# Naming ScalarE's function tables, and reading the shift weights from PSUM, in a decoder layer whose order is written by a planner

## The chip, the cores and the metric

The kernel runs on one core of a Trainium2 chip. Its time is the device time of one execution in microseconds (us). A core has a matrix engine (TensorE, PE in the profile), a vector engine (VectorE, DVE), an engine for functions such as exp and sqrt (ScalarE, ACT), a general engine (GpSimd, POOL) and a sync engine (SP) that only issues transfers. Each engine runs its own list of instructions in the order in which the program gives them; semaphores make one engine wait for another. Matrix products land in a memory of their own, PSUM, of which the kernel uses eight banks of 128x512 float32; the other memory on the core is SBUF, and in this kernel GpSimd reads and writes only that.

## The reference

One decoder layer over x of 16 sequences, 256 steps, 256 channels, all float32. It has three parts, each followed by a residual sum and a layer norm:

```python
# 1. gated cosine/sine recurrence
z = causal_conv4(x @ in_proj_w) + conv_b          # values, gate, 32 scores
p_w = exp(clip(score_scale * s_raw, -20, 20)) * time_weight
re, im = cumsum(p_w * poly(x5) * cos(x5 * theta)), cumsum(p_w * poly(x5) * sin(x5 * theta))
y = rms_normalised(re, im) @ (W_re, W_im)
x = layernorm(x + (y * silu(gate)) @ out_proj_w)
# 2. attention over shifts in time, 16 heads of 16 channels
corr = irfft(rfft(Q) * conj(rfft(K))).mean(channels)
w, idx = top_k(corr, 5);  w = softmax(w)
x = layernorm(x + sum_k(w[k] * V rolled by idx[k]) @ Wo + bo)
# 3. eight experts, forward and inverse branch
h = gelu(Q @ router_w1.T + b1);  weights = softmax(h @ router_w2.T + b2)
out = sum_k(weights[k] * ((Q @ V[k]) * cumsum(K @ W[k])) @ U[k].T) / n_valid
x = layernorm(x + out)
```

## The kernel before, in words

The 16 sequences are worked on as 8 pairs. For every pair the program notes seven stages (lines 1202 to 1204): `front` and `body` (part 1), `context`, `back` and `attention` (part 2), `router` and `experts` (part 3). Nothing is issued while a stage is noted. `Later` (line 68) and `Work.note` (line 186) put each instruction into a list with an estimate of its duration, the tiles that it touches and what it depends on. `Work.run` (line 424) then plans: `forward` (line 267) hands out work engine by engine by rank and readiness, `backward` (line 414) makes new ranks from the latest starts, this is done three times, and the order with the shortest planned span is kept. `give` (line 435) issues the instructions in that order. All of them are issued from line 438, so the profile puts nearly everything on L438, and an operation is known by its tiles.

Three things of the planner bear on the change.

- **Tables.** The planner takes ScalarE to hold one set of functions at a time. `SETS` (line 120) tells the planner which functions share one: Exp 0, Sin and Silu 1, Gelu 2, Sqrt 3. When the function kind changes, `forward` adds 1283 ns (lines 372 and 373). The kernel issues no load of a table; whatever builds the program puts one in where a function needs it.
- **Places.** A tile takes one of its tag's buffers when its first instruction is planned, and gives it back after its last. For a tile in a PSUM pool with several buffers, `after` (filled at line 259) lists the SBUF tiles that its readers use; `room` (line 289) lets the first product into the bank only if there are places for those as well, and `takes` (line 409) only if what the readers depend on is already planned.
- **Locks.** Two-input VectorE and GpSimd instructions on SBUF are planned so that they don't overlap (`lock`, lines 177 and 376). One with a PSUM operand is planned without that.

The planner keeps no order between two engines that only read the same PSUM tile.

The part of the data path that changes is in attention. For each pair `choose` (line 955) picks five shifts for 32 heads, transposes their weights (`w_t_ps`, `wT`) and turns them into weights per frequency by 12 small products into a bank `w_f_ps`, one of the four banks of the pool `f_ps` that also carries `c_ps`, `v_ps`, `u_ps`, `h_ps`, `kv_ps`, `q_ps`, `roll_ps` and others. ScalarE copies its 96 columns to SBUF, tile `wf`. `rolled` (line 1002), once for each sequence of the pair, multiplies the spectrum `vf` of V by these weights into tile `t`: two 128x256 products on VectorE, two on GpSimd, then two sums on VectorE, and 16 products into two `roll_ps` banks. There is one buffer for `t`, shared with `pp`: the second sequence of a pair can write its `t` only when the first one's `roll_ps` products have read theirs. `layernorm` (line 559) uses Sqrt, `front` Exp and Silu, `body` Sin and Sqrt, `choose` Exp, `router` Gelu and Exp.

Of the kernel before, what the change touches and what calls it, by code (L numbers as in the profile page):

```python
# [18 lines left out]
PSUM = bass.MemoryType.PSUM  # L19
HBM = bass.MemoryType.DRAM  # L20

P = 128
# [5 lines left out]
NH, DK = 16, 16  # L28
# [20 lines left out]
EARLY, SLABS, XT_BUFS, ZC_BUFS, KBUFS, VBUFS, X_BUFS = 3, 18, 1, 6, 2, 3, 9  # L49
AHEAD = range(1, NP)  # L50
PH_BUFS = 2
# [62 lines left out]
class Work:  # L114
# [3 lines left out]


    SETS = {AF.Exp: 0, AF.Sin: 1, AF.Silu: 1, AF.Gelu: 2, AF.Sqrt: 3}  # L120
    AHEAD = 40000.0
    LEAD = {"PE": 0, "DVE": 85, "ACT": 103, "POOL": 40, "SP": 0}
    LATE = {"PE": 33, "DVE": 35, "ACT": 35, "POOL": 80, "SP": 40}
# [62 lines left out]
    def note(self, eng, op, issue, args, kw):  # L186
# [21 lines left out]
        if op == "activation":  # L208
            o.table = self.SETS.get(args[2])
        for ap in ins + [out]:  # L210
# [26 lines left out]
    def prepare(self):  # L237
        for o in self.ops:
            if o.eng == "PE":
                cells, begin, end = {}, 0.0, 0.0  # L240
                for d, group in o.mm:
                    begin = max([begin] + [cells.get(g, 0.0) for g in group])
                    cells.update((g, begin + d) for g in group)
                    end, begin = max(end, begin + d), begin + 13
                o.dur, o.lat = end, end + 165
            for q in o.pre:
                q.then.append(o)
        self.slots, self.turn, self.kind, self.after = {}, {}, {}, {}
        for name, (t, users) in self.tiles.items():
            users[:] = dict.fromkeys(users)  # L250
            self.slots.setdefault(t.tag, t.tag_meta.bufs)


            kind = t.tag, t.source_name if t.source_name in self.shares else None
            self.kind[name] = None if t.space == PSUM and t.tag_meta.bufs > 1 else kind
            if self.kind[name]:
                self.turn.setdefault(kind, []).append(name)
            to = [n for o in users if o.eng != "PE" for n in o.tiles if n != name] if not self.kind[name] else []
            self.after[name] = [n for n in dict.fromkeys(to) if self.tiles[n][0].space != PSUM]

    def gap(self, q, o, raw):

# [4 lines left out]
    def forward(self, rank, late=None):  # L267
        need = {o: len(o.pre) for o in self.ops}

        ready = {o: max(0.0, late[o] - self.AHEAD) if late and o.fetch else 0.0 for o in self.ops}  # L270
        can = {e: sorted((rank[o], o.k, o) for o in self.ops if o.eng == e and not o.pre) for e in self.LEAD}
# [161 lines left out]
        self.give(best[1], best[2])  # L433

    def give(self, order, starts):
        for o in order:
            for call, args, kw in o.parts:
                call(*args, **kw)  # L438

# [2 lines left out]
def decoder_kernel(ctx: ExitStack, tc: tile.TileContext, a: dict, out: bass.AP):  # L442
    nc = tc.nc
    ctx.enter_context(tc.manual_schedule())
    work = Work(1)
    work.shares.update({"raw": 11, "inv": 2, "ks": 6, "ct": 2, "bothc": 1, "specc": 2, "e": 8, "wb": 3, "h": 2, "lT": 1, "lg8": 1, "fwT": 2, "x": 3, "dx": 2, "x2": 4})
    V, S, G, T, Y = (
        Later(work, name, eng)
# [38 lines left out]
    def split(ps, n=2):  # L487
        return ps.rearrange("p (c d) -> p c d", c=n)
# [96 lines left out]
    spectra_of = {}  # L585
# [191 lines left out]
    ps = f_bank("bv_ps")  # L777
# [110 lines left out]
    def context(p):  # L888

        for b in (2 * p, 2 * p + 1):  # L890
# [3 lines left out]
            cf = transform(ct, G, "c", slab)  # L894
            if p in AHEAD:
                kf, vf = (slab([P, 2, D], "ks") for _ in range(2))
# [58 lines left out]
    def choose(prod):  # L955


        NHP = 2 * NH
        ps = f_bank("corr_ps")
        for i in range(3):  # L960
            T.matmul(ps[:NHP, :L], prod[:, i, :], c_corr[:, i, :], start=i == 0, stop=i == 2)
        T.matmul(ps[:NHP, L : L + 1], prod[:, 0, :], c_mean, start=True, stop=True)
        corr = new(at, [NHP, L], "corr")
        top = new(at, [NHP, 8], "top")
        m8 = new(at, [NHP, 8], "m8")
        rest = new(at, [NHP, L], "rest")
        S.copy(corr, ps[:NHP, :L])
        S.copy(top[:, 0:1], ps[:NHP, L : L + 1])
        V.max(m8, corr)
        V.tensor_copy(m5[:, :TOPK], m8[:, :TOPK])  # L970
        V.match_replace(rest, m5, corr, -FAR)
        V.tensor_scalar(m8, m8, top[:, 0:1], None, ALU.add)
        V.tensor_scalar(top[:, 1:2], m8[:, 0:1], -1.0, None, ALU.mult)
        V.tensor_tensor(top[:, 2:3], top[:, 1:2], top[:, 0:1], ALU.add)
        S.activation(m8, m8, AF.Exp, bias=top[:, 1:2])
        S.activation(corr, corr, AF.Exp, bias=top[:, 2:3])
        V.tensor_reduce(top[:, 3:4], m8[:, :TOPK], AX.X, ALU.add)
        V.reciprocal(top[:, 4:5], top[:, 3:4])
        V.scalar_tensor_tensor(corr, rest, -FAR, corr, ALU.is_equal, ALU.mult)

        we = new(at, [NHP, 2, P], "we")
        r = top[:, 4:5]
        S.activation(corr[:, P:], corr[:, P:], AF.Identity, scale=r)
        V.scalar_tensor_tensor(we[:, 0, :], corr[:, :P], r, corr[:, P:], ALU.mult, ALU.add)
        V.scalar_tensor_tensor(we[:, 1, :], corr[:, :P], r, corr[:, P:], ALU.mult, ALU.subtract)
        ps = f_bank("w_t_ps")
        for c in range(2):
            T.transpose(ps[:, c * NHP : (c + 1) * NHP], we[:, c, :], ident[:NHP, :NHP])
        wT = new(at, [P, 2, NHP], "wT")
        S.copy(wT, split(ps[:, : 2 * NHP]))  # L990
        ps = f_bank("w_f_ps")
        for i in range(3):
            for o in range(2):
                T.matmul(
                    ps[64 * o : 64 * o + 64, i * NHP : (i + 1) * NHP], f_roll[:, o, i, :], wT[:, o, :],
                    start=True, stop=True,
                )
        wf = new(at, [P, 3, NHP], "wf")
        S.copy(wf, split(ps[:, : 3 * NHP], 3))
        return wf  # L1000

    def rolled(b, vf, wf):

        lo = (b % 2) * NH

        def times(eng, dst, f, kind):
            eng.tensor_tensor(
                dst.rearrange("p (h d) -> p h d", d=DK),
                vf[:, f, :].rearrange("p (h d) -> p h d", d=DK),
                wf[:, kind, lo : lo + NH].unsqueeze(2).to_broadcast([P, NH, DK]),  # L1010
                ALU.mult,
            )

        t = new(at, [P, 4, D], "pp", name="t")
        times(V, t[:, 0, :], 0, 0)
        times(G, t[:, 1, :], 1, 2)
        times(G, t[:, 2, :], 1, 1)
        times(V, t[:, 3, :], 0, 2)
        V.tensor_tensor(t[:, 0, :], t[:, 0, :], t[:, 1, :], ALU.add)
        V.tensor_tensor(t[:, 2, :], t[:, 2, :], t[:, 3, :], ALU.subtract)  # L1020
        banks = [f_bank("roll_ps") for o in range(2)]
        work.apart()
        work.joins = True
        for cb in range(2):
            for i in range(2):
                for o in range(2):
                    rows = slice(64 * o, 64 * o + 64)
                    T.matmul(
                        banks[o][:, cb * P : (cb + 1) * P], t[rows, 2 * i, cb * P : (cb + 1) * P], c_roll[rows, i, :],
                        start=i == 0, stop=i == 1,  # L1030
                    )
        work.joins = False
        work.apart()
        aT = new(at, [P, 2, L], "aT")
        for o in range(2):
            S.copy(aT[:, o, :], banks[o][:, :L])

        ps = f_bank("wo_ps")
        for o in range(2):
            for cb in range(2):  # L1040
                T.matmul(ps[:, o * D : (o + 1) * D], aT[:, o, cb * P : (cb + 1) * P], wo[:, cb, :], start=cb == 0, stop=cb == 1)
        dx = xs[b]
        V.tensor_tensor(dx, dx, split(ps), ALU.add)
        x = xs[b] = new(mx, [P, 2, D], "x", X_BUFS, "x2")
        G.tensor_tensor(x[:, 0, :], dx[:, 0, :], dx[:, 1, :], ALU.add)
        G.tensor_tensor(x[:, 1, :], dx[:, 0, :], dx[:, 1, :], ALU.subtract)

    def attention(p):
        place = lambda f: work.place("att", p, f)
        work.rank = place(0.0)  # L1050
        prod = new(at, [P, 3, 2 * NH], "prod", 2)
        pair = (2 * p, 2 * p + 1)
        for b in pair:
            work.rank = place(0.15 * (b % 2))
            spectra(b, prod)
        work.rank = place(0.4)
        wf = choose(prod)
        for b in pair:
            work.rank = place(0.7 + 0.15 * (b % 2))
            rolled(b, spectra_of[b][1], wf)  # L1060
        work.rank = place(1.0)
        layernorm(at, "al", [xs[b][:, c, :] for b in pair for c in range(2)], b_eps4)

# [283 lines left out]
```

## Time and profile before

| what | us |
|---|---|
| time, median of 3 runs | 868.76 (867.9 to 875.24) |
| the profiled execution | 868.91 |
| its span | 867.1 |
| PE busy | 812.6 (94%) |
| DVE busy | 712.3 (82%) |
| ACT busy | 593.4 (68%) |
| POOL busy | 273.4 (32%) |

The mean clock granted to TensorE was 0.985 of full speed. The span is what the trace covers; the profiled execution's own time is 1.8 us longer. Busy times overlap and don't add up to the span. In a group's line the fields are: engine, operation, output and input tiles, shapes, count, then total busy us and mean ns of one instruction, then the idle time of that engine just before these instructions with the releaser that ended most of it. In a line of waits the three numbers are the total us, how often, and the longest one.

### The profile page before, as it was taken

How to read it: one execution, taken by the hardware profiler on the slowest of the kernel's cores; microseconds unless marked ns; L12 is line 12 of the kernel's file. 1: busy time of each engine (PE TensorE's matmuls, PEld its weight loads, DVE VectorE, ACT ScalarE, POOL GpSimd, SP SyncE). 2: the span in 40 equal slices, each digit the busy share in tenths (PEclk: the TensorE clock that was granted, in tenths of full speed). 3: DMA queues.
4: the chain of work that ended last, by engine and by line, in shares of the span. 5: the costliest groups of instructions: out<-in, count | busy, mean ns of one | idle time of the engine just before them, and what ended most of it. 6: DMA issues, size and time to landing. Idle time of an engine off the chain costs nothing.

```text
span 867.1 us, 12898 instructions
## 1 busy us (share of the span) xinstructions
PE 812.6 (94%) x4628; PEld 464.9 (54%) x4628; DVE 712.3 (82%) x1248; ACT 593.4 (68%) x884; POOL 273.4 (32%) x301
## 2 busy tenths in 40 slices
PE   4799998899989999999999999899999999999994
PEld 2355553554435655565446654565566457556553
DVE  6499799779999999999899999999999985472331
ACT  3769968489978689748878787889875824532301
POOL 8522386535113123250232321353334221130000
PEclk9899998999999999999999999999999999999997
DMA  8963657255726442744075435535544340040130
GB/s 274 325 129 71 182 168 222 77 146 134 185 52 154 102 106 65 179 121 99 25 175 142 101 83 133 140 82 108 149 97 96 69 116 1 3 119 1 39 83 24
DMA packets 52304, 99.16 MB, mean 114 GB/s; under 512 B 6592, under 2 KB 18912, under 8 KB 52240
## 3 DMA queue, kind: packets, MB, share of 16 engines
q1 hardware_dynamic: 42640, 67.65, 34.0%
q0 software_dynamic: 9600, 30.69, 10.9%
q8 instruction: 36, 0.59, 0.3%
q14 instruction: 28, 0.23, 0.1%
HBM read 28.06 MB, written 11.53 MB: 46 GB/s over the span
## 4 chain that ended last, share of the span: by engine, by line
PE 54%; DVE 22%; ACT 9%; issue 6%; DMA 6%; SPq 2%; POOL 1%; POOLq 0%; DVEq 0%; ACTq 0%
PE u_ps L438 9%; PE v_ps L438 9%; PE c_ps L438 9%; DVE cs L438 7%; PE h_ps L438 5%; DVE sn L438 3%; PE kv_ps L438 3%; DVE zc L438 3%; PE in_ps L438 3%; PE wo_ps L438 2%; PE out_ps L438 2%; DMA sn<-zc 2%; PE q_ps L438 2%; SPq L438 2%; PE y L438 2%
## 5 line engine op out<-in xcount | busy, mean ns | idle before, releaser
L438 ACT ACT_TABLE_LOAD x96 | 123.2, 1283 | 41.4 <-DVE flmv L438 36.5
L438 PE MATMUL v_ps<-fxT,w_v 128*128 128x512 f32 x256 | 119.5, 600 | 1.2 <-ACT e L438 1.2
L438 PE MATMUL c_ps<-fcT,w_c 128*128 128x512 f32 x256 | 119.0, 599 | 0.7 <-DVE e L438 0.7
L438 PE MATMUL u_ps<-u_o,e 128*128 128x256 f32 x512 | 116.7, 381 | 0.6 <-DVE e L438 0.6
L438 PEld LDWEIGHTS u_ps<-u_o,e 128*128 128x128 f32 x512 | 95.7, 190 | 19.0 <-issue 6.3
L438 DVE TENSOR_TENSOR_SCAN cs<-again,cs 128x1024 f32<-128x1024 bf16 x32 | 82.0, 2564 | 0.0
L438 DVE SCALAR_TENSOR_TENSOR zc<-in_ps,pv,zc 128x255 f32<-128x255 f32 (+4 forms) x144 | 75.9, 557 | 2.5 <-ACT zc L438 2.2
L438 DVE TENSOR_TENSOR_SCAN sn<-again,sn 128x1024 f32<-128x1024 bf16 x32 | 76.5, 2390 | 0.1
L438 PEld LDWEIGHTS c_ps<-fcT,w_c 128*128 128x128 f32 x256 | 46.8, 190 | 54.1 <-issue 46.7
L438 PEld LDWEIGHTS v_ps<-fxT,w_v 128*128 128x128 f32 x256 | 46.6, 190 | 52.8 <-issue 46.5
L438 PE MATMUL kv_ps<-Wkv,specc 128*128 128x512 f32 x128 | 61.2, 616 | 7.7 <-ACT specc L438 5.5
L438 PE MATMUL in_ps<-xT,in_proj_w 128*32 128x256 f32 (+1 forms) x576 | 64.7, 423 | 3.5 <-DVE zc L438 3.4
L438 POOL TENSOR_TENSOR pp<-qf,kf 128x512 f32<-128x512 f32 (+1 forms) x32 | 50.9, 1608 | 49.0 <-ACT qf L438 39.9
L438 PE MATMUL h_ps<-fxT,w_h 128*128 128x512 f32 x128 | 60.3, 601 | 0.0
L438 DVE TENSOR_TENSOR e<-e,v_ps 128x512 f32<-128x512 f32 x64 | 43.0, 674 | 14.9 <-PE v_ps L438 14.8
L438 POOL TENSOR_TENSOR t<-vf,wf 128x256 f32<-128x256 f32 x32 | 29.3, 934 | 80.3 <-ACT wf L438 66.2
L438 POOL DMA_DIRECT2D out<-x x16 | 11.8, 735 | 134.2 <-ACT x L438 133.4
L438 DVE TENSOR_TENSOR sn<-sn,ge 128x1024 f32<-128x1024 f32 x32 | 41.5, 1297 | 10.7 <-ACT w_v L438 4.5
L438 ACT ACTIVATE sq<-cs 128x1024 f32<-128x1024 f32 x32 | 33.8, 1055 | 22.6 <-DVE cs L438 22.3
L438 ACT ACTIVATE sn<-sn,theta_col 128x512 f32<-128x512 f32 x64 | 44.5, 715 | 5.9 <-DMA sn<-zc 5.8
L438 PEld LDWEIGHTS in_ps<-xT,in_proj_w 128*32 128x32 f32 (+1 forms) x576 | 28.5, 123 | 34.6 <-issue 23.8
L438 ACT ACTIVATE ge<-sn 128x1024 f32<-128x1024 f32 x32 | 33.8, 1056 | 18.0 <-DVE sn L438 13.3
(219 smaller groups left out, 1622.8 us busy)
## 6 DMA issues: line engine op xcount, KB each, us to landing
sn<-zc SPq DMA_DIRECT2D x64, 256.0 KB
ge<-g SPq DMA_DIRECT2D x64, 256.0 KB
wb<-fwT SPq DMA_DIRECT2D x64, 256.0 KB
xT<-in_xT SPq DMA_DIRECT2D x8, 512.0 KB
ct<-in_ctx SPq DMA_DIRECT2D x16, 256.0 KB
x<-in_x POOLq DMA_DIRECT2D x16, 256.0 KB, 5.2
ph<-sc SPq DMA_DIRECT2D x64, 64.0 KB
vh<-sv SPq DMA_DIRECT2D x32, 128.0 KB
```

Source lines behind the costliest of these rows:

```text
L438: call(*args, **kw)
```

## The change

- `give` keeps track of the set of functions that the planner assumes, and issues a load of that set by name ahead of every instruction where the set changes. The four names are in a new tuple `TABLES`. Sin and Silu are both under "silu_and_others".
- `choose` returns the PSUM bank of the weights beside the SBUF copy. In `rolled` the VectorE products read the weights from the bank, the GpSimd products from the copy. The copy stays.
- `after` lists, of tiles with one tag, no more than the tag has buffers. `w_f_ps` now has both sequences' `t` among its readers' tiles, and there is one buffer for them.

```diff
     SETS = {AF.Exp: 0, AF.Sin: 1, AF.Silu: 1, AF.Gelu: 2, AF.Sqrt: 3}
+    TABLES = "exp_and_others", "silu_and_others", "gelu_and_others", "sqrt_and_others"
...
-            self.after[name] = [n for n in dict.fromkeys(to) if self.tiles[n][0].space != PSUM]
+            to = [n for n in dict.fromkeys(to) if self.tiles[n][0].space != PSUM]
+
+            self.after[name] = [
+                n for k, n in enumerate(to)
+                if sum(self.tiles[q][0].tag == self.tiles[n][0].tag for q in to[:k]) < self.tiles[n][0].tag_meta.bufs
+            ]
...
     def give(self, order, starts):
+        table = None
         for o in order:
+            if o.table is not None and o.table != table:
+                table = o.table
+                self.scalar.preload_act_table_set(self.TABLES[table])
             for call, args, kw in o.parts:
                 call(*args, **kw)
...
     work = Work(1)
+    work.scalar = nc.scalar
...
         S.copy(wf, split(ps[:, : 3 * NHP], 3))
-        return wf
-
-    def rolled(b, vf, wf):
+        return wf, split(ps[:, : 3 * NHP], 3)
+
+    def rolled(b, vf, wf, wf_ps):
...
-                wf[:, kind, lo : lo + NH].unsqueeze(2).to_broadcast([P, NH, DK]),
+                (wf_ps if eng is V else wf)[:, kind, lo : lo + NH].unsqueeze(2).to_broadcast([P, NH, DK]),
...
-            rolled(b, spectra_of[b][1], wf)
+            rolled(b, spectra_of[b][1], *wf)
```

## The prediction

> **What bounds the kernel now.** I began with the page: busy times, the forty slices, the shares of the chain that ended last.
>
> ```profile
> span 867.1 us, 12898 instructions
> PE 812.6 (94%) x4628; PEld 464.9 (54%) x4628; DVE 712.3 (82%) x1248; ACT 593.4 (68%) x884; POOL 273.4 (32%) x301
> ...
> DVE  6499799779999999999899999999999985472331
> ...
> PE 54%; DVE 22%; ACT 9%; issue 6%; DMA 6%; SPq 2%; POOL 1%; POOLq 0%; DVEq 0%; ACTq 0%
> ```
>
> TensorE is busy all but 54.5 us of the span. The busy times by stretches of 50 us place those: 17.1 us in the first 50, 18.0 between 50 and 350, 7.0 between 350 and 700, none between 700 and 800, 12.4 in the last 67. Only the 25 us in the middle and the tail are open to this change; the start waits for transfers. In the middle most slices have VectorE at 90% and more, and the chain goes back and forth between TensorE and VectorE. ScalarE has a third of its time free, but the chain passes through it for 9%.
>
> Then ScalarE's groups and its list in order of time (start, length, operation, and in brackets its idle time before).
>
> ```profile
> L438 ACT ACT_TABLE_LOAD x96 | 123.2, 1283 | 41.4 <-DVE flmv L438 36.5 <-DVE cs L438 2.0 <-PEq L1337 0.7
> ```
>
> ```profile
> 409.14 1.34 ACT L438 ACTIVATE sn<-sn,theta_col 128x512 f32<-128x512 f32 x2
> 410.50 1.28 ACT L438 ACT_TABLE_LOAD   x1
> 411.79 0.63 ACT L438 ACTIVATE zc<-zc 128x512 f32<-128x512 f32 x1
> ...
> 857.67 1.28 ACT L438 ACT_TABLE_LOAD   x1 [36.54 <-DVE flmv L438]
> 858.97 0.30 ACT L438 ACTIVATE flrs<-flmv,bias_c 128x4 f32<-128x4 f32 x1
> ```
>
> The load at 410.50 stands ahead of Silu, though the function before it was Sin. After a load for Silu, Sin runs without one (at 32.13, 312.80, 544.72 and four more times); the reverse needs one. So Silu's table serves both, and another one is fetched for Sin alone. The pattern of 410.50, a load from Sin to Silu, occurs six times: at 99.96, 216.89, 233.15, 410.50, 494.96, 672.26. The load at 857.67 comes after the 36.5 us in which ScalarE waited for the last layer norm's sums: it stands behind the wait.
>
> Last, VectorE's groups and the waits.
>
> ```profile
> L438 DVE TENSOR_TENSOR t<-vf,wf 128x256 f32<-128x256 f32 x32 | 20.3, 673 | 5.5 <-ACT wf L438 4.3 <-PE roll_ps L438 1.0
> L438 DVE TENSOR_TENSOR qf<-q_ps,b_dc 128x256 f32<-128x256 f32 x16 | 6.6, 411 | 10.3 <-PE q_ps L438 8.8 <-ACT qf L438 1.4
> ```
>
> ```profile
> POOL t L438 <- ACT wf L438: 66.2, 6, 22.9
> ...
> ACT qf L438 <- DVE qf L438: 7.6, 3, 5.0
> ...
> DVE t L438 <- ACT wf L438: 4.3, 2, 3.3
> ```
>
> The products that the change touches take 673 ns on average (402 to 846), the same shape with a PSUM operand 411 (391 to 425). GpSimd runs its own two products at the same moment, and the slow ones are slow together.
>
> **The tables.** With Silu's set named for Sin too, the six loads go: 6 x 1.283 = 7.7 us of ScalarE. The chain in order of time shows which of them the end depends on: those at 410.50 and 672.26 are pieces of it; at 99.96 and 216.89 it runs through kv_ps on TensorE, at 233.15 through the ge<-g transfer, at 494.96 through VectorE's sn. So 2 x 1.28 = 2.6 us on the path. What is late next at both is VectorE or TensorE, which had been waiting for ScalarE about 1 us there (TensorE 1.2 us for e at 680).
>
> A rule speaks for more. The Trainium skill, "ScalarE: Activation LUTs", section "What ACT_TABLE_LOAD costs", puts a switch at 2.66 us, a load of 1.283 and a drain of 1.38. By that the six would be worth 16.0 us, 5.3 on the path. The list shows 10 to 20 ns between the end of the instruction before and the load, and as much behind it; there is no drain to save, and I go by the row.
>
> The other 90 loads stay if the order stays, at the same 1.283. What changes is where they stand: issued as an instruction of its own ahead of the function, a load needn't wait for the function's input. The idle time ahead of loads is 41.4 us, 36.5 at the end, so nearly all other loads followed busy work and gain nothing. At the end the load fits into the idle time, and Sqrt, reciprocal, four normalisations and the output transfer all come 1.28 us earlier. At 422.95 another 1.28 of 2.0 us could hide, but the chain there is on wo_ps: 0.
>
> At the start one load may be added: the first function, Abs, belongs to no set in the planner's list, gets its load at 0.74 without a name, and the named one comes behind it, ahead of the first Exp at 7.17. From 0 (if it is dropped) to 1.28 us. ScalarE waits 1.98 us for sc_ps soon after, VectorE would start its little chain on sp 0.3 late. I take +0.3.
>
> **The weights from PSUM.** 32 products by 673 - 411 = 262 ns: 8.4 us less of VectorE. GpSimd's two beside them (614 ns at least, 934 on average) get quicker as well, but the two sums need GpSimd's products, at least 2 x 0.61 = 1.2 us after wf, while VectorE's own would be done after 0.82: in its fixed order VectorE may stand idle for 0.4 us, in 16 places up to 6.4 of the 8.4. The chain goes through these products on VectorE in three of eight pairs (near 156, 246 and 510 to 516): 12 x 0.262 = 3.1 us. From 0 to 8.4, I take 2.5.
>
> The wait of VectorE for the copy wf (4.3 us, two places) looks as if it went away. I count nothing. ScalarE's and VectorE's reads of q_ps write different halves of qf, yet in none of the 16 cases do they overlap, and ScalarE waits for VectorE (7.6 us) or VectorE for ScalarE (1.4). The Trainium skill, "PSUM — Partial Sum Buffer", section "PSUM bank collisions raise a hardware error", says that two engines may not even read one bank at once, and so must be ordered. The first product will wait for the copy as before, or the copy for two products (0.82 us), and with it everything queued on ScalarE and GpSimd's products. By the row and the rule 0 or a loss below 0.8 a pair; without them 8 x 0.25 = 2 us gain, the copy's own length. 0.
>
> The bank: w_f_ps is now held until the second sequence's products have read it. From the end of each copy to the end of the second pair of products the list gives 11.0, 16.2, 9.4, 6.9, 6.3, 5.6, 7.6 and 5.5 us, together 68 us in which the products for the experts have three banks instead of four, and one while two roll_ps banks are out. Today TensorE hardly ever waits for a bank: v_ps for e 1.2 us, c_ps for e 0.7. The bound above is one group of four products (1.9 us) per pair, 15 us; below, 0, as VectorE empties a bank in 0.67 us while TensorE fills one in 1.7 to 1.9. I take 0.1 us per pair: +0.8.
>
> `after`: the shortened list matters only for w_f_ps, whose readers now include two tiles of a one-buffer tag; elsewhere the list is as before. It costs no instruction.
>
> Sum: -2.6 -1.3 +0.3 -2.5 +0.8 = -5.3 us. The profiled execution took 868.91, its span 867.1; the median is 868.76, so the sum stands against either: 861.8 for the span, 863.5 for the time.
>
> **What the sum can't see.** The planner sees different dependencies, no lock for 32 products and a longer hold, so every later decision may fall otherwise, for work that has nothing to do with the change. The ranks and stage positions are not altered with it. That is the main uncertainty, to both sides.
>
> **The rivals.**
> *The freed time adds up* (854): in the stretches between 50 and 700 us, where TensorE idles 25 us, VectorE is 8.4 us lighter and ScalarE 7.7. If 0.8 of those 16.1 us reach the end, with 1.3 of the tail, it is 14 us. For it: the chain crosses DVE and ACT for 31%. Against: only 3 of 8 pairs and 2 of 6 loads lie on it.
> *Hidden anyway* (868): TensorE is the bound, each gain turns into a longer wait for it, and only the tail stays, less the load at the start: -1.3 +0.3. For it: from 550 on the chain is nearly all TensorE.
> *The bank* (880): between w_f_ps and the second sequence's products the four-bank pool is short. The place is the roll_ps stretch of each pair; a stall of 2 us there, one group of products, in eight pairs is 16, less 5 of the gains: +11. From 6.1 / 8 = 0.8 us per pair on, the change is slower than before; from 1.8 on by over 1%. For it: the eight holds, and that roll_ps takes two banks. Against: VectorE's 0.67 against TensorE's 1.9. An order that the planner draws less well ends here too.
> *The names don't do what they say* (about 900): if the automatic loads stayed beside the named ones, 90 x 1.283 = 115 us would come to ScalarE, 709 us busy, as full as VectorE now. A quarter of it on the path is +30. The load's own operation on the profile would show it at once.
>
> **Chances.** The forecast (860 to 867 around 863.5) 0.43; the freed time adds up 0.24; hidden 0.09; the bank 0.22; the names 0.02. Over 1% (8.7 us, about what a measurement of this kernel can tell from no change) faster is below 860.1: 0.24 and 0.06 of the forecast's edge, 0.30. Slower, above 877.4: 0.21 of the bank and the names. The rest, 0.49, lies between. The range goes down to 849 (all of the 16.1 us and the tail give 851, GpSimd's quicker products a little more) and up to 882, past the bank's price; about 0.18 is left out.
>
> **What would show it.** Table loads 90 or 91 if the order is kept, none from Sin to Silu, each at 1283 ns; the last load ending before the last flmv; t<-vf,w_f_ps at about 411 ns; VectorE near 704 us busy, ScalarE near 586; waits between wf and t still there. The bank would show as TensorE waiting for e or x ahead of c_ps, v_ps or u_ps within some 10 us of w_f_ps. I am wrong if loads stay at 96 or more, if VectorE's gain comes back as waits for POOL t, or if TensorE's idle time in the middle moves by more than 10 us in stretches that hold neither a removed load nor a t.

## The result, and the profile after

The kernel after takes 874.28 us (median of 20 runs), the kernel before 870.28 beside it: a ratio of 1.0047, with a 95% interval of 1.0032 to 1.0062. It is slower by about 4 us, where 5.3 us less were forecast. The wide range went up to 882 us and holds the result; the forecast and the side that it took do not.

Both edits did what they were to do. The page of after, its busy times and the shares of its chain:

```profile
span 871.2 us, 12903 instructions
PE 813.1 (93%) x4628; PEld 463.3 (53%) x4628; DVE 700.6 (80%) x1248; ACT 596.0 (68%) x886; POOL 253.5 (29%) x301
...
PE 45%; DVE 23%; ACT 15%; issue 7%; DMA 5%; SPq 2%; POOL 1%; POOLq 0%; DVEq 0%; ACTq 0%
```

VectorE's busy time fell by 11.7 us, TensorE's stayed, and yet the span grew by 4.1 us. TensorE is on the chain for 45% where it was 54%, ScalarE for 15% where it was 9%. Then the groups of the products and of the loads, in after:

```profile
L448 DVE TENSOR_TENSOR t<-vf,w_f_ps 128x256 f32<-128x256 f32 x32 | 12.0, 412 | 2.9 <-PE roll_ps L448 2.5 <-ACT wf L448 0.3
```

```profile
L446 ACT ACT_TABLE_LOAD x97 | 124.5, 1283 | 1.7
```

The 32 products take 412 ns, as the row of qf had said (411). There are 97 named loads (L446 is the line that issues them) and the one that the program builder still puts ahead of Abs. None stands between Sin and Silu, though the order goes from Sin to Silu eight times. ScalarE is 596.0 us busy, not the 586 that were forecast: this order has 97 changes of set where before's has 90. The idle time ahead of named loads is 1.7 us, where it was 41.4; the load for the last layer norm is done before the wait, as ScalarE's list at the end of after shows:

```profile
826.48 1.28 ACT L446 ACT_TABLE_LOAD   x1
863.02 0.30 ACT L448 ACTIVATE flrs<-flmv,bias_c 128x4 f32<-128x4 f32 x1 [35.26 <-DVE flmv L448]
```

But 97 named loads can't be before's order: with the six gone there would have been 90 (91 with the one at the start, 98 here; 96 or more was one of the prediction's signs of being wrong). Nearly everything stands elsewhere. The chain of before, in a stretch of some 9 us (start, length, what):

```profile
604.70 1.91 PE v_ps L438 x4
606.61 1.72 PE c_ps L438 x4
608.33 1.73 PE wo_ps L438 x8
610.05 3.43 PE c_ps L438 x8
```

and the chain of after, in the same stretch:

```profile
604.96 1.28 ACT L446
606.25 1.16 ACT cs L448
607.43 1.23 DVE cs L448
608.66 0.60 DVE e L448
...
609.49 0.96 ACT ge L448
610.46 1.28 ACT L446
611.76 1.06 ACT sn L448
612.81 1.97 ACT x L448 x4
```

Before, TensorE was never without work there. After, the chain goes through the angles of part 1 on ScalarE and VectorE, and two loads of tables are pieces of it. The stretch from 50 to 700 us as a whole says how much that is. The lines below are from the table of busy times by stretch (stretch and length, then busy us and counts of PE, PEld, DVE, ACT, POOL, then clock and transfers); before's first, after's second:

```profile
50.00:700.00 650.00, 625.09 (x3822) 356.37 (x3818) 607.03 (x993) 516.75 (x754) 221.06 (x220) 0.99 0.50 122
```

```profile
50.00:700.00 650.00, 622.30 (x3814) 352.07 (x3813) 591.85 (x985) 519.26 (x756) 200.16 (x218) 1.00 0.48 120
```

TensorE stands idle for 24.9 us of it before and 27.7 us after, while VectorE has 15 us less to do. The start, 17.1 us idle before, is 18.8 after.

### The profile page after: what moved, and what is told of

It is laid out like the page before. It is cut to its first block, busy times and chain, and to the rows that moved or that the text cites. A ratio compares the mean times of both kernels' runs of the same rounds, so it can differ in the third digit from the quotient of the medians.

```text
span 871.2 us, 12903 instructions
## 1 busy us (share of the span) xinstructions
PE 813.1 (93%) x4628; PEld 463.3 (53%) x4628; DVE 700.6 (80%) x1248; ACT 596.0 (68%) x886; POOL 253.5 (29%) x301
## 4 chain that ended last, share of the span: by engine, by line
PE 45%; DVE 23%; ACT 15%; issue 7%; DMA 5%; SPq 2%; POOL 1%; POOLq 0%; DVEq 0%; ACTq 0%
PE u_ps L448 9%; PE c_ps L448 6%; PE v_ps L448 6%; DVE cs L448 6%; DVE sn L448 4%; PE h_ps L448 4%; ACT L446 3%; PE kv_ps L448 3%; ACT cs L448 3%; ACT sn L448 3%; DVE zc L448 3%; SPq L448 2%; DVE e L448 2%; PE dft_ps L448 2%; DMA xT<-in_xT 2%
## 5 line engine op out<-in xcount | busy, mean ns | idle before, releaser
L448 DVE SCALAR_TENSOR_TENSOR zc<-in_ps,pv,zc 128x255 f32<-128x255 f32 (+3 forms) x144 | 76.4, 558 | 2.8 <-ACT zc L448 2.5
L448 DVE TENSOR_TENSOR_SCAN cs<-again,cs 128x1024 f32<-128x1024 bf16 x32 | 73.7, 2304 | 0.0
L448 DVE TENSOR_TENSOR e<-e,v_ps 128x512 f32<-128x512 f32 x64 | 43.0, 675 | 21.3 <-PE v_ps L448 20.3
L448 POOL TENSOR_TENSOR t<-vf,wf 128x256 f32<-128x256 f32 x32 | 24.4, 779 | 122.0 <-ACT wf L448 88.4
L448 POOL TENSOR_TENSOR pp<-qf,kf 128x512 f32<-128x512 f32 (+1 forms) x32 | 40.7, 1290 | 55.3 <-ACT qf L448 53.2
L448 DVE TENSOR_TENSOR sn<-sn,ge 128x1024 f32<-128x1024 f32 x32 | 41.4, 1293 | 15.5 <-ACT sn L448 12.0
L448 POOL TENSOR_TENSOR g<-g,zc 128x512 f32<-128x512 f32 x16 | 22.7, 1420 | 105.1 <-ACT g L448 99.5
L448 DVE SCALAR_TENSOR_TENSOR cs<-cs,sn 128x1024 f32<-128x1024 f32 x32 | 41.4, 1295 | 6.9 <-ACT cs L448 6.9
```

## Experiments

My theory after seeing this (O): the edits save what was worked out, and the order that the planner drew for the changed dependencies costs more than that. Its first rival (E): the edits themselves cost, by the load at the start, by VectorE's and ScalarE's reads of one bank, or by the bank that is held longer. A second one (B) came up with the results: that it is the longer hold which forces a worse order on the planner. Times are medians of each run; "before" ran beside each group and was 870.3 to 870.4.

| kernel | order | tables | VectorE reads | us | ratio to before |
|---|---|---|---|---|---|
| names_old_order | before's | named | SBUF | 865.75 | 0.9939 (0.9915 to 0.9962) |
| old_order_psum_first | before's | named | PSUM for 16 of 32 | 863.46 | 0.9920 (0.9892 to 0.9949) |
| order_alone | after's | unnamed | SBUF for 28 of 32 | 882.02 | 1.0132 (1.0102 to 1.0162) |
| new_order_sbuf | after's | named | SBUF for 28 of 32 | 876.95 | 1.0074 (1.0047 to 1.0101) |
| psum_auto_loads | after's | unnamed | PSUM | 879.55 | 1.0100 (1.0066 to 1.0134) |
| after | after's | named | PSUM | 874.28 | 1.0047 (1.0032 to 1.0062) |
| one_ns_in_the_plan | a third | unnamed | SBUF | 885.61 | 1.0177 (1.0146 to 1.0208) |
| late_34 | a fourth | unnamed | SBUF | 881.56 | 1.0124 (1.0098 to 1.0150) |
| placed_anew | a fifth | named | PSUM | 873.42 | 1.0038 (1.0025 to 1.0050) |
| placed_anew_b | a sixth | named | PSUM | 869.70 | 0.9995 (0.9980 to 1.0010) |
| sbuf_placed_anew | a seventh | named | SBUF | 869.95 | 0.9995 (0.9979 to 1.0010) |
| sbuf_placed_anew_b | an eighth | named | SBUF | 868.65 | 0.9979 (0.9966 to 0.9993) |

### The names alone, in before's order

```diff
     def give(self, order, starts):
+        table = None
         for o in order:
+            if o.table is not None and o.table != table:
+                table = o.table
+                self.scalar.preload_act_table_set(self.TABLES[table])
```

> Only the tables are named, the plan and the order are those of before. Theory O (the new order costs, the edits save): 4 us less than before, from 2.6 us of two loads on the path and 1.3 us at the end, so a ratio of 0.994 to 0.998, with 90 or 91 loads and none from Sin to Silu. Theory E (the edits themselves cost, here the named loads with the one added at the start): a ratio of 1.000 or more.

4.6 us less than the kernel before by the medians, 5.3 by the ratio of 0.9939, which is clear of 1. In this trace the group of named loads and the stretch from 50 to 700 us read:

```profile
L441 ACT ACT_TABLE_LOAD x90 | 115.5, 1283 | 1.6
```

```profile
50.00:700.00 650.00, 628.79 (x3864) 358.71 (x3863) 612.04 (x999) 510.51 (x751) 220.58 (x221) 0.99 0.50 122
```

With the unnamed one ahead of Abs, 91 loads, five fewer than before's 96. TensorE's idle time between 50 and 700 us falls from 24.9 to 21.2 us, 3.7 us; the rest of the gain is at the end. E falls for the names. The place of the load that stood at 410.50 now reads:

```profile
408.03 1.33 ACT L443 ACTIVATE sn<-sn,theta_col 128x512 f32<-128x512 f32 x2
409.26 0.62 ACT L443 ACTIVATE zc<-zc 128x512 f32<-128x512 f32 x1
```

Silu starts 0.10 us before Sin has ended; with the load between them it started 1.31 us after. So a load there cost 1.41 us, a little more than its row. The first load is the one thing that they cost, as allowed for (its price was not measured by itself): ScalarE's list at the start of this kernel has both,

```profile
0.74 1.28 ACT L443 ACT_TABLE_LOAD   x1 [0.74 <-PEq L1343]
6.71 0.20 ACT L443 ACTIVATE sp<-pv 128x1 f32<-128x1 f32 x1 [4.69 <-DMA pv<-in_pv]
6.93 1.28 ACT L441 ACT_TABLE_LOAD   x1
8.22 0.20 ACT L443 ACTIVATE sp<-sp 128x1 f32<-128x1 f32 x1
```

### After's order with before's instructions

After's plan is made, with its dependencies on the bank, but the products are issued with the SBUF copy and no table is named:

```diff
-                self.scalar.preload_act_table_set(self.TABLES[table])
...
+            if eng is V and b not in (10, 14):
+                call, args, kw = work.last.parts[-1]
+                read = wf[:, kind, lo : lo + NH].unsqueeze(2).to_broadcast([P, NH, DK])
+                work.last.parts[-1] = call, args[:2] + (read,) + args[3:], kw
```

In two of the eight pairs (sequences 10 and 14) after's order has a product of the first sequence ahead of the copy, so these 4 products keep reading the bank.

> The order of after, with before's instructions: tables unnamed, VectorE's products read the SBUF copy, except for 4 of the 32 that this order puts ahead of the copy and that go on reading PSUM. Theory O: slower than after, since the order is kept and both savings are taken away; 878 to 882 us, a ratio to before of 1.010 to 1.015. Theory E: near before, a ratio of 1.003 or less.

882.02 us, 1.3% over before: as theory O had it, and far from E. All but those 4 products do what they did before, and those 4 are quicker (414 ns on average), so the order alone costs 11.5 us at the ratio's middle, 8.9 to 14.1 by its interval. The stretch between 50 and 700 us of this kernel:

```profile
50.00:700.00 650.00, 615.94 (x3757) 348.44 (x3755) 589.43 (x975) 517.29 (x750) 194.90 (x216) 1.00 0.49 120
```

TensorE stands idle for 34.1 us there, 9.2 more than before. This is where the forecast gain went. The waits that grew most are not for the products that the change touches:

```profile
PE u_ps L444 <- ACT h L444: 3.6, 1, 3.6
PE dft_ps L444 <- DVE dx L444: 3.1, 3, 2.0
PE corr_ps L444 <- DVE prod L444: 2.6, 3, 1.3
```

In before the second of these is 0.8 us and the other two 0.1 at most.

### Each edit taken back, in after's order

Without the names:

```diff
-                self.scalar.preload_act_table_set(self.TABLES[table])
```

> After without the names: its order and its reads of PSUM, the loads put in by the program builder. This order goes from Sin to Silu eight times, so eight loads or 10.3 us of ScalarE more than after, and the last load again behind the wait. Theory O: 2 to 6 us over after, a ratio to before of 1.007 to 1.012. Theory E, if the names cost: below after, a ratio of less than 1.004.

5.3 us above after by the medians, a ratio of 1.0100: inside what O expected. One figure in it was off. I had counted eight more loads; the trace has 101 loads against 98, for a load comes back only where the Sin ahead of Silu had itself followed another set. Four did; where Silu had come before Sin, its table was still there. The load that names add at the start is gone as well.

Without the bank, but with the names (the second part of the edit of order_alone):

> After with 28 of the 32 VectorE products reading the SBUF copy again, order and names kept. VectorE becomes some 7 us busier (28 x 0.26). Theory O: 1 to 4 us over after, a ratio to before of 1.006 to 1.010. Theory E, if reading PSUM costs: below after, a ratio of less than 1.004.

2.7 us above after by the medians; the ratios, 1.0074 and 1.0047, have intervals that overlap, so the size is loose and the sign likely. Here six of the eight pairs give the bank back right after the copy, and that made nothing faster: neither the longer hold nor the shared reads of the bank cost anything that shows against the almost 8 us that VectorE has more to do (708.3 to 700.6 busy). What the hold does to the order that the planner draws can't be seen here, since the order is kept.

### Before's order, with as much of the bank as it allows

In before's order the four-bank pool is full at some point between the copy and the second sequence's products in six of the eight pairs, so they can't all read PSUM. The products of the first sequence can:

```diff
+            if eng is V and b % 2 == 0:
+                call, args, kw = work.last.parts[-1]
+                read = wf_ps[:, kind, lo : lo + NH].unsqueeze(2).to_broadcast([P, NH, DK])
+                work.last.parts[-1] = call, args[:2] + (read,) + args[3:], kw
```

> Before's plan and order, tables named, and VectorE's two products for the first sequence of each pair read PSUM without the planner's knowledge; those for the second sequence read the SBUF copy, since in this order the bank is needed by others before they come. Theory O: the saving of the names stays (0.994) and 16 products get some 0.26 us quicker, of which at most 2 us show: a ratio of 0.991 to 0.995, 863 to 866 us. Theory E (reading PSUM costs by a wait that wasn't there): a ratio above 0.996.

863.46 us, a ratio of 0.9920: the fastest by its median, and faster than the kernels before and after. Over names_old_order it gains 0.2%, less than the intervals can part. The two groups of products on VectorE in this kernel show that the operand's place does it, with GpSimd working on the same tile in both:

```profile
L443 DVE TENSOR_TENSOR t<-vf,wf 128x256 f32<-128x256 f32 x16 | 10.1, 674 | 1.6 <-PE roll_ps L443 1.5
...
L443 DVE TENSOR_TENSOR t<-vf,w_f_ps 128x256 f32<-128x256 f32 x16 | 5.8, 404 | 3.3 <-ACT wf L443 3.2
```

And VectorE still waits for the copy wf before its first product, though it doesn't read it: 3.2 us once.

### Does any disturbance of the plan cost as much?

Two kernels issue before's instructions with one number of the planner moved by 1 ns:

```diff
+        elif op == "tensor_tensor" and n == D and not psum:
+            d = 150 + 1.04 * n + 1
```

> Before, with one number of the planner moved: its estimate for a two-input VectorE instruction of 256 columns in SBUF is 1 ns longer. No instruction, no dependency and no buffer changes, only the order that the planner draws. Theory O in its wide form (before's places fit before's estimates so closely that any disturbance draws a worse order): slower than before, a ratio of 1.005 to 1.020. Theory B (it is the longer hold of the bank that makes the new order worse): within 0.3% of before, as nothing is held longer.

```diff
-    LATE = {"PE": 33, "DVE": 35, "ACT": 35, "POOL": 80, "SP": 40}
+    LATE = {"PE": 33, "DVE": 34, "ACT": 35, "POOL": 80, "SP": 40}
```

> A second neutral disturbance of before: the planner's delay from another engine to VectorE is 34 ns instead of 35, no instruction changes. Theory O wide: slower than before, a ratio of 1.004 to 1.018. Theory B, or one_ns_in_the_plan as a freak: within 0.3% of before.

885.61 and 881.56 us, 1.8% and 1.2% over before. Nothing is held longer, no wait is added, no data are read elsewhere. The kernel with 1 ns more even has 87 loads of tables instead of 96 and ScalarE 11 us lighter:

```profile
PE 819.3 (93%) x4628; PEld 465.6 (53%) x4628; DVE 711.7 (81%) x1248; ACT 582.4 (66%) x875; POOL 266.8 (30%) x301
```

So a disturbance of the plan is enough for a loss of this size, and the loss of after needs no cause of its own in the bank. It is not the same loss in all its parts: in these two kernels some 7 us of it is busy time of TensorE (819.3 and 819.7 us for 812.6), in order_alone 1.3 us (813.9). Why the same matrix products keep TensorE busy for longer there was not found.

### Can the gain be had back by placing the stages anew?

Both kernels are after with other values of PLACES, found by small steps that shortened the plan:

```diff
-    "front": (0.8, 1.05, 3.35, 3.25, 3.85, 4.6, 6.2, 5.8, 7.6),
+    "front": (0.8, 0.9, 3.1, 3.85, 3.85, 4.4, 6.1, 6.1, 8.0),
...
-    "att": (0, -3.1, -1.9, -2.55, -2.65, 0.8, 0.9, 2.55, 3.4),
+    "att": (0.5, -1.8, -2.45, -2.55, -1.35, 0.05, 0.25, 2.3, 3.4),
```

> After, with other stage places (PLACES), found for after's dependencies by trying small steps and keeping what shortens the planner's own plan. Theory O wide: the savings come out once the order is as good as before's; a ratio of 0.988 to 0.996, 860 to 867 us. Theory B (three banks are too few while the weights are held): no order gets below before, a ratio of 0.999 or more.

> As the kernel placed_anew, with places from another start of the search, whose plan is as short to within 0.2%. Theory O wide: a ratio of 0.988 to 0.998. Theory B: 0.999 or more. The difference between the two shows how far equally long plans lie apart on the chip.

1.0038 and 0.9995. The second is 4.6 us under after, but neither comes clear below before, and O in its wide form had expected 0.996 or less of the first and 0.998 or less of the second: two misses, and what B had foretold. Two controls tell B apart. They have before's dependencies, so no bank is held longer, and names; their PLACES come from a search of the same kind.

> The control for placed_anew: before's dependencies, VectorE reads the SBUF copy and no bank is held longer, tables named, and other stage places found by the same search from a start far from before's. Its plan is 0.5% longer than that of placed_anew by the planner's own count. Theory B (the held bank keeps new orders from being good): a ratio below 0.996, as in names_old_order, as nothing is held. Theory O wide (a plan's length tells only roughly what the chip does, and before's order is a lucky one): at or above placed_anew's 1.004.

> A second control, from another start, with a plan 0.3% longer than the first control's. Theory B: a ratio below 0.998. Theory O wide: 1.004 or more.

0.9995 and 0.9979. B wanted them down at 0.996 and 0.998 or less; O wanted 1.004 or more. Neither number was met by the first, the second just meets B's (its interval reaches 0.9993). So O in its wide form missed all four of these forecasts. Against names_old_order, which differs from them in the order alone, they lose 0.4 to 0.6%, so a new order costs without the hold as well. (In sbuf_placed_anew the granted clock was 0.972 to 0.980 in its 14 runs, 0.979 or more in all runs of the other kernels; how much of its loss is that was not parted.) Against the two with the hold they gain 0 to 0.6%, and these four orders lie apart by as much among themselves: 0.4% between the two with the hold. The two with the hold also have the quicker products, and by the planner's own count (given below) their plans are shorter than the other two, so they should have come first. A part for the hold, of some tenths of a per cent and by the planner's count up to about 1%, is not excluded; it is left open.

## Why the prediction was wrong, step by step

**The tables: right in kind, sized a little low.** -2.6, -1.3 and +0.3 made -3.6 us. Measured, -5.3 in before's order (the ratio's middle, 0.9939; -3.3 to -7.4) and 0.53% in after's order (1.0100 to 1.0047). The choice of the trace's row over the drain that the Trainium skill adds ("ScalarE: Activation LUTs", section "What ACT_TABLE_LOAD costs") gave 3.6; with the drain, the path's 5.3 and the tail's 1.3, less 0.3 at the start, would have given some 6.3. The measured gain lies between, and its interval holds both. The lists show no drain: nearly every load in them stands within 10 to 25 ns of the instruction before it. What the row leaves out is the 0.10 us by which two functions overlap without a load: 1.41 us each, 2.8 for the two on the path where 2.6 stood. More of the six loads may have mattered than these two, as TensorE's idle time fell by 3.7 us.

**The weights from PSUM: right in the group, roughly right in the sum.** 412 ns for 411, and 20.3 us for all 32 became 12.0, 8.3 less where 8.4 were worked out. That VectorE lost 11.7 us in all has another source: order_alone, with the products as they were but for four, is already at 706.8 busy, so some of it comes with the order. Forecast -2.5 +0.8; in after's order the edit is worth 0.27% with names (1.0074 to 1.0047) and 0.32% without (1.0132 to 1.0100), some 2.3 to 2.8 us for 28 products, with intervals that overlap.

**The wait for the copy: right.** It counted nothing, and it stayed: in after, twice it is the copy that waits for the products.

```profile
ACT wf L448 <- DVE t L448: 1.2, 2, 0.9
...
580.21 0.54 PE L448 MATMUL w_f_ps<-wT,f_roll 128*64 128x32 f32 x12
581.25 0.75 DVE L448 TENSOR_TENSOR t<-vf,w_f_ps 128x256 f32<-128x256 f32 x2
582.09 0.24 ACT L448 COPY wf<-w_f_ps 128x96 f32<-128x96 f32 x1 [0.26 <-DVE t L448]
```

The first line is from the waits; the others are pieces of the engines' lists in order of time, put together, around one of the two. The bank is written until 580.7, VectorE reads it from 581.25, ScalarE's copy begins when VectorE is done, and GpSimd's products begin after the copy.

**The bank: not seen on the chip.** TensorE's waits for VectorE's or ScalarE's e and aT ahead of c_ps and v_ps came to 3.2 us after, 1.9 before (first two lines before, last two after):

```profile
L438 PE MATMUL v_ps<-fxT,w_v 128*128 128x512 f32 x256 | 119.5, 600 | 1.2 <-ACT e L438 1.2
L438 PE MATMUL c_ps<-fcT,w_c 128*128 128x512 f32 x256 | 119.0, 599 | 0.7 <-DVE e L438 0.7
...
L448 PE MATMUL v_ps<-fxT,w_v 128*128 128x512 f32 x256 | 120.7, 602 | 0.7 <-DVE e L448 0.7
L448 PE MATMUL c_ps<-fcT,w_c 128*128 128x512 f32 x256 | 119.0, 598 | 2.4 <-DVE e L448 1.3 <-ACT aT L448 1.2
```

The rival's mechanism, 2 us in each pair, is not there. That its total, 880, was nearer than mine is luck as far as its own stall goes; but its last sentence put an order drawn less well under it, and that is what came.

**The order: the step that failed.** I wrote that every later decision may fall otherwise, called it the main uncertainty "to both sides", and put 0 into the sum. It is 11.5 us to one side (order_alone). Set in, the sum reads 11.5 for the order, -4.6 for the names in it (0.53%), -2.3 for the bank (0.27%), together 4.6 us; measured are 4.1 (0.47%). That the two agree is no test: the terms are differences of the same few kernels, and the 0.5 us left over says only that the two edits hardly depend on each other.

That the side could have been known is the lesson. The planner says it before anything runs. Its own length of the plan, the `span` that `Work.run` keeps, comes out of the planning in each kernel alone: 836.2 us for before and 852.4 for after, 1.9% more, though it counts the same duration for every instruction of both. order_alone ran 1.3% longer. For one_ns_in_the_plan and late_34 it is 851.5 and 846.2, 1.8 and 1.2% more, just what was measured. The price that I put at 0 could be read off there. Why the plan grows is not shown beyond this: the stage places in the kernel are fine-grained numbers, one for each pair and stage, and they go together with this planner, these estimates and these dependencies. The profile of before shows what that order achieves: TensorE without a gap from 700 to 800 us and 7 us idle between 350 and 700. Moving one number by 1 ns loses 1.2 to 1.8% (shown for two numbers). Of the seven other orders, five were run with instructions that before's order was run with, all but 4 products of order_alone, and all five were slower; the other two, with all products reading PSUM, were slower than before's order with half of them. That the places were once picked for the time they gave is a likely reason, but was not shown. A re-drawn order should have been priced as a loss, by the difference of the two plans, with a chance of little gain.

## What to carry to other kernels

If an order is written out by a planner whose parameters fit it closely, an edit that changes a dependency, a lifetime or an estimate pays twice: its own price, and that of a new order; price the second as a loss unless it is shown otherwise. First try the edit with the order kept, by changing what is issued and not what is planned; here that gave 0.9920, the best of all, against 1.0047 for the same two ideas planned anew. And compare the planned lengths first, for large differences alone: plans 1.2 to 1.9% longer than before's gave orders 1.2 to 1.8% slower, but the plans of placed_anew and placed_anew_b, 0.3 and 0.1% shorter than before's (833.7 and 834.9 us), ran 1.0 and 0.6% behind names_old_order, which has before's order, and those of the two controls, 838.3 and 840.5 us, 0.6 and 0.4% behind it.

## What was unexpected of the hardware

Two-input products on VectorE with one operand in PSUM stayed at 404 to 412 ns on average while GpSimd multiplied beside them; with both in SBUF they averaged 592 to 690 ns in the traces of nine kernels. It is GpSimd's work beside them that makes the difference: with both operands in SBUF, too, the one to five products (in eight of these traces) that hardly any product of GpSimd overlapped took 393 to 424 ns on average, those overlapped for nine tenths of their time or more 676 to 822. GpSimd's own products gained as well: in after's order, with names, they took 852 ns on average beside SBUF reads (28 of 32) and 779 beside PSUM reads; in before's order 900, and 805 with the bank read for half of VectorE's products. I had named this gain of the other engine and given it no number.
